# The last four row blocks of a graph-attention kernel: search order, piece size, store size and the place of four small maxima

## The chip, the cores and the metric

The kernel runs on one core of a Trainium2 chip. The metric is the device time of one launch in microseconds. The kernel before took 246.74 us (median of five runs, 246.5 to 248.25).

## What is computed

The reference is one graph-attention layer with a residual and a layer norm:

```python
ht  = (h @ W).reshape(N, 4, 512).transpose(1, 0, 2)
e   = leaky_relu(src[:, :, None] + dst[:, None, :], 0.01) + adj_mat[None]
att = softmax(e, axis=-1)
out = layernorm(h + einsum('hij,hjd->hid', att, ht).mean(axis=0))
```

Here N is 4096, h is 4096x512, adj_mat is 4096x4096, all float32. The entries of adj_mat reach 1e9, and the other term of e is small beside the gaps between a row's largest entries. In almost any row the softmax is therefore one at the row's largest adjacency entry and zero elsewhere, and the layer becomes: find the column of the largest entry of each row, fetch that row of x, multiply it by the mean of the four heads' weights, add the row's own x, and normalize.

## The kernel before, in words

`leading_rows` does this short form for all rows, and checks by the gap between a row's two largest entries that the short form holds; `general`, the full softmax, runs for blocks where it does not, behind a branch that these inputs do not take.

The rows are taken in NB = 32 blocks of 128. Row p * 32 + ib belongs to block ib and lies on partition p, so that four neighbouring blocks of x or of the output are 8 KB in one piece on each partition. A block of the adjacency is 128x4096 float32, 2 MB. For block ib the stages are:

- **Load** (`load_adj`, L105): one to four DMAs on the queue of SyncE (SP), as `pieces` (L102) says: four for blocks 0, 28 and 31, two for 29 and 30, one for the others. `LATE` is 28. Six buffers hold blocks; loads run five blocks ahead.
- **Segment maxima** (`segment_maxima`, L149): VectorE (DVE) takes the maximum of each of the 64 segments of 64 columns, by reductions over halves or quarters of the block (L155). Blocks that come in one piece are reduced in halves.
- **Segment** (`find_segment`, L160): DVE takes the eight largest of the 64 maxima and the place of the largest (L162, L164); GpSimd (POOL) turns this into a row number (L166), gathers that segment's 64 entries from the adjacency in HBM (the `lead` gather, L168), and multiplies for the column's start (L173).
- **Column** (`find_column`, L186): DVE takes the eight largest entries within the segment (`find_inner`, L184, needed only for the gap check at the very end) and the place of the largest (L190); POOL adds it to the start (L192) and gathers the row of x (the `y` gather, L178). Block 31 has its column found in the whole row (`find_column_in_row`, L198), without the lead gather, which is still made for the check.
- **Product** (`turn`, L201; `products`, L213): TensorE (PE) transposes y (L205), ScalarE (ACT) copies it out (L207), PE multiplies it by the mean weights (L218). For blocks below 28 and for 31 PE also adds the block's own x by an identity matmul (`residual`, L211).
- **Norm**: for most blocks ACT computes the sums (`stats`, L230 and L232) and applies the result (`finish`, L241), with a power on POOL for each pair of blocks (`rstd`, L235 to L237). For blocks 28 to 31 `finish_last` (L243) does it on DVE, with a square root on ACT (L254).
- **Store** (L258): on SP's queue, except the last block's, which ACT issues.

The order on each engine is the order of the program, written out by hand. Step t of the loop (L354) issues the load of block t + 5, the first part of block t's segment maxima, the column of block t - 2, the remaining maxima, the segment of block t, the product of block t - 3, the sums of block t - 4 and, on even steps, the results of blocks t - 6 and t - 5. "The first part" is `middle` quarters (L358): two in all steps but the last, one in step 31.

What comes after the loop is written out (L393 to L431): the load of x for blocks 28 to 31 in one DMA; the stores of blocks 0 to 23 in fours and of 24 and 25 singly; the column of block 30 and of block 31; then, mixed on the engines, the products of blocks 29, 30 and 31, the norms of 28 to 31, the gap check, and the stores of 26 to 31. The gap check has a scalar bound, computed in three parts (`bound`, L309): part 0 takes a maximum on DVE (L313) and transposes it on PE (L315), part 1 ends with a tiny matmul (L320), part 2 is on DVE. `test` (L327) compares on DVE, `count` (L337) sums on PE.

All DMAs issued by SP and ACT share eight completion semaphores in turn; a DMA is issued when the one eight before it has landed. The same holds for POOL's gathers with eight others.

Of the kernel before, what the change touches and what calls it, by code (L numbers as in the profile page):

```python
# [65 lines left out]
def leading_rows(ctx, tc, x, adj, W, a, out, ident, v, n_bad, any_bad):  # L66
# [7 lines left out]
    nc = tc.nc  # L74
    N, D = x.shape
    H = a.shape[0]
    KB, NB, S = D // P, N // P, N // E
    AHEAD = 5
    Q = 4
    PIECES = 4  # L80
    LATE = NB - Q
# [18 lines left out]
    adj_t = {}  # L100

    def pieces(ib):  # L102
        return PIECES if ib in (0, LATE, NB - 1) else 2 if ib > LATE else 1

    def load_adj(ib):  # L105
        if 0 <= ib < NB:
            t = adj_t[ib] = adj_pool.tile([P, N], F32, name="adj_t")
            n = pieces(ib)
            for k in range(n):
                nc.sync.dma_start(t[:, ts(k, N // n)], adj_rows[ib][:, ts(k, N // n)])  # L110

    def load_x(lo, n):
        nc.sync.dma_start(hold[:, ds(lo, n), :], x_rows[:, ds(lo, n), :])
# [35 lines left out]
    def segment_maxima(ib, lo, hi):  # L149

        if lo == 0:
            seg_of[ib] = small.tile([P, S], F32, name="seg")
        n = max(pieces(ib), 2)
        for k in range(lo * n // PIECES, hi * n // PIECES):
            nc.vector.tensor_reduce(  # L155
                seg_of[ib][:, ts(k, S // n)],
                adj_t[ib][:, ts(k, N // n)].rearrange("p (s e) -> p s e", e=E), axis=AX.X, op=OP.max,
            )

    def find_segment(ib):  # L160
        seg = seg_of.pop(ib)
        nc.vector.max(out=top[:, ib, :], in_=seg)  # L162
        at = small.tile([P, 8], U32, name="at")
        nc.vector.max_index(at, top[:, ib, :], seg)  # L164
        row = small.tile([P, 1], U32, name="row")
        nc.gpsimd.tensor_tensor(row, at[:, 0:1], first[:, ib : ib + 1], op=OP.add)  # L166
        lead = small.tile([P, E], F32, name="lead")
        nc.gpsimd.indirect_dma_start(  # L168
            out=lead, out_offset=None, in_=adj_segs,
            in_offset=bass.IndirectOffsetOnAxis(ap=row[:, :1], axis=0),  # L170
        )
        start = at_of[ib] = small.tile([P, 1], U32, name="start")
        nc.gpsimd.tensor_tensor(start, at[:, 0:1], width, op=OP.mult)  # L173
        lead_of[ib] = lead

    def gather_rows(ib, col):
        y = y_t[ib] = rows.tile([P, D], F32, name="y", bufs=4)
        nc.gpsimd.indirect_dma_start(  # L178
            out=y, out_offset=None, in_=x,
            in_offset=bass.IndirectOffsetOnAxis(ap=col[:, :1], axis=0),  # L180
        )

    def find_inner(ib):
        nc.vector.max(out=inner[:, ib, :], in_=lead_of[ib])  # L184

    def find_column(ib):  # L186
        if ib != NB - 2:
            find_inner(ib)
        within = small.tile([P, 8], U32, name="within")
        nc.vector.max_index(within, top[:, ib, :], lead_of[ib])  # L190
        col = small.tile([P, 1], U32, name="col")
        nc.gpsimd.tensor_tensor(col, at_of.pop(ib), within[:, 0:1], op=OP.add)  # L192
        gather_rows(ib, col)
# [7 lines left out]
    def turn(ib):  # L201
        y = y_t.pop(ib)
        tp = psum.tile([P, KB, P], F32, name="tp", bufs=2)
        for kb in range(KB):
            nc.tensor.transpose(tp[:, kb, :], y[:, ts(kb, P)], ident)  # L205
        yt = yt_of[ib] = rows.tile([P, KB, P], F32, name="yt")
        nc.scalar.copy(yt, tp)  # L207
# [26 lines left out]
    def rstd(i):  # L234
        nc.gpsimd.tensor_scalar(sd[:, i], sd[:, i], 1.0 / D, EPS, op0=OP.mult, op1=OP.add)  # L235
        nc.gpsimd.tensor_tensor(sd[:, i], sd[:, i], power[:, : i.stop - i.start], op=OP.pow)  # L236
        nc.gpsimd.tensor_mul(nm[:, i], nm[:, i], sd[:, i])  # L237

    def finish(ib):
        i = slice(ib, ib + 1)  # L240
        nc.scalar.activation(hold[:, ib, :], o_ps.pop(ib), AF.Identity, bias=nm[:, i], scale=sd[:, i])  # L241

    def finish_last(ib, residual):  # L243

        o = o_ps.pop(ib)
        if residual:
            nc.vector.tensor_add(hold[:, ib, :], o, hold[:, ib, :])
            o = hold[:, ib, :]
        st = small.tile([P, nc.vector.BN_STATS_DIM], F32, name="st", bufs=2)
        nc.vector.bn_stats(st, o)  # L250
        mv = small.tile([P, nc.vector.BN_AGGR_DIM], F32, name="mv", bufs=2)
        nc.vector.bn_aggr(mv, st)
        r = small.tile([P, 1], F32, name="r", bufs=2)
        nc.scalar.activation(r, mv[:, 1:2], AF.Sqrt, bias=eps)  # L254
        nc.vector.reciprocal(r, r)
        nc.vector.tensor_scalar(hold[:, ib, :], o, mv[:, 0:1], r, op0=OP.subtract, op1=OP.mult)

    def store(queue, lo, n):  # L258
        queue.dma_start(out_rows[:, ds(lo, n), :], hold[:, ds(lo, n), :])

    def mean_of_heads(kb):
        o = psum.tile([P, D], F32, name="o")
        for h in range(H):
            nc.tensor.matmul(o, ident, hold[:, w_at + kb * H + h, :], start=(h == 0), stop=(h == H - 1))  # L264
        nc.scalar.activation(w_sum[:, kb, :], o, AF.Copy, scale=1.0 / H)  # L265
# [5 lines left out]
    def turn_a():  # L271
        tp = psum.tile([P, KB, P], F32, name="tp", bufs=2)
        for k in range(KB):
            nc.tensor.transpose(tp[:, k, : 2 * H], a_rows[:, ts(k, P)], ident[: 2 * H, : 2 * H])
        nc.scalar.copy(at_d, tp[:, :, : 2 * H])

    def turn_w(kb, h):
        tp = psum.tile([P, KB, P], F32, name="tp", bufs=2)
        for k in range(KB):
            nc.tensor.transpose(tp[:, k, :], hold[:, w_at + kb * H + h, ts(k, P)], ident)  # L280
        wt = rows.tile([P, KB, P], F32, name="wt")
        nc.scalar.copy(wt, tp)  # L282
        return wt
# [25 lines left out]
    def bound(part):  # L309

        if part == 0:
            xm = once.tile([P, 1], F32, name="xm")
            nc.vector.tensor_reduce(xm, xx, axis=AX.X, op=OP.max)  # L313
            px = of_bound[0] = psum.tile([1, P], F32, name="px", bufs=1)
            nc.tensor.transpose(px, xm, ident)  # L315
        elif part == 1:
            nc.vector.tensor_reduce(xg, of_bound[0], axis=AX.X, op=OP.max)
            nc.scalar.activation(xg, xg, AF.Sqrt)
            pb = of_bound[1] = psum.tile([P, 1], F32, name="px", bufs=1)
            nc.tensor.matmul(pb, ones[0:1, :], xg, start=True, stop=True)  # L320
        else:
            nc.vector.tensor_mul(lead_by, of_bound[1], vn)
            nc.vector.tensor_scalar(lead_by, lead_by, 1.05, 110.0, op0=OP.mult, op1=OP.add)
# [28 lines left out]
    COLUMN, PROJECT, STATS, FINISH = 2, 3, 4, 6  # L352

    for t in range(NB):  # L354
        if t in x_at:
            load_x(*x_at[t])
        load_adj(t + AHEAD)
        middle = 1 if t == NB - 1 else 2  # L358
        segment_maxima(t, 0, middle)
        if t >= COLUMN:  # L360
            find_column(t - COLUMN)
        segment_maxima(t, middle, PIECES)
        pair = t >= FINISH and t % 2 == 0
        if pair:
            rstd(slice(t - FINISH, t - FINISH + 2))
        find_segment(t)
        if t < 2:
            mean_of_heads(t)
        elif t == 2:
            mean_of_heads(2)  # L370
            mean_of_heads(3)
        if t == 0:
            turn_a()
        turned = [(*vectors[0], turn_w(*vectors.pop(0))) for _ in range(vectors_at.get(t, 0))]
        if t == 16:
            head_norms()
        ib = t - PROJECT
        if ib >= 0:
            turn(ib)
            if ib < LATE:  # L380
                residual(ib)
        for some in turned:
            head_vector(*some)
        if ib >= 0:
            products(ib)
        if t >= STATS:
            stats(t - STATS)
            row_norm(t - STATS)
        if pair:
            finish(t - FINISH)  # L390
            finish(t - FINISH + 1)

    load_x(LATE, NB - LATE)  # L393
    for lo in range(0, NB - 2 * Q, Q):
        store(nc.sync, lo, Q)
    for ib in range(NB - 2 * Q, NB - FINISH):
        store(nc.sync, ib, 1)
    find_column(NB - 2)
    rstd(slice(NB - FINISH, NB - FINISH + 2))
# [4 lines left out]
    products(NB - 3, 0, KB - 1)  # L404
    finish(NB - FINISH)
    finish(NB - FINISH + 1)
    bound(0)
    finish_last(NB - 4, True)
    find_inner(NB - 2)
    find_inner(NB - 1)  # L410
    turn(NB - 2)
    products(NB - 3, KB - 1, KB)
    residual(NB - 1)
# [252 lines left out]
```

## Time and profile before

| | |
|---|---|
| median of five runs | 246.74 us |
| the profiled execution: its time / its span | 246.95 / 244.9 us |
| DVE busy | 186.3 us, 76% |
| PE busy | 201.1 us, 82% |
| ACT busy / POOL busy | 109.8 / 97.3 us |
| moved by DMA | 97.76 MB at a mean of 399 GB/s |
| segment maxima (L155) | 70 reductions, 2268 ns of a half, 1.2 us of a quarter |
| y gathers (L178) | 32, 958 ns each on POOL, 6.3 to 9.3 us from issue to landing |
| lead gathers (L168) | 32, 964 ns on POOL, 5.4 to 7.6 us to landing |
| stores of four blocks / of one block on SP's queue | 6 of 1024 KB / 7 of 256 KB |
| last instruction before the end of the span | store of block 31, issued at 239.94 us |

Times within a profile are microseconds from the start of the span. The timeline gives the start, the duration, the engine, the line and the tiles of each instruction, and in brackets how long its engine had been idle and what released it. The "DMA" row of the page gives the share of time that the 16 DMA engines were busy, in forty slices of 6.1 us.

### The profile page before, as it was taken

What the parts mean: (1) busy time and instruction counts of PE and PEld (TensorE: products, weight loads), DVE (VectorE), ACT (ScalarE), POOL (GpSimd) and SP (SyncE); (2) the same over time, 40 slices, a digit from 0 to 9 for tenths busy, and PEclk for the clock granted to TensorE, in tenths of its full rate; (3) what the DMA queues carried; (4) which work ended last, traced back from release to release, by engine and by line L of the source; (5) the groups of instructions that cost most, each with busy time, mean ns of one, the idle gap of its engine ahead of it and who ended that gap; (6) DMA issues with size and microseconds to landing.
All of it is one profiled execution on the core that took longest, in us unless ns stands there. A gap on an engine that the chain in (4) does not pass through costs nothing.

```text
span 244.9 us, 2481 instructions
## 1 busy us (share of the span) xinstructions
PE 201.1 (82%) x677; PEld 101.6 (41%) x678; DVE 186.3 (76%) x300; ACT 109.8 (45%) x266; POOL 97.3 (40%) x213
## 2 busy tenths in 40 slices
PE   0189958999999899999959979599868989858970
PEld 0035416555565555555334424243323433324520
DVE  2635785399689887999589969985998998977651
ACT  2012004055747474757646655247444845656110
POOL 1102422326425543645254636453545464742000
PEclk9999799999999999999979999799999999979997
DMA  6999999999999999999999999999999999999961
GB/s 248 439 423 412 424 427 417 422 410 423 420 412 415 411 421 420 422 402 426 424 410 419 422 419 418 408 416 415 425 409 399 407 403 406 407 425 427 412 241 55
DMA packets 13988, 97.76 MB, mean 399 GB/s; under 512 B 2184, under 2 KB 2184, under 8 KB 7824
## 3 DMA queue, kind: packets, MB, share of 16 engines
q1 hardware_dynamic: 10224, 87.82, 86.8%
q0 software_dynamic: 3584, 9.44, 9.8%
q10 hardware_dynamic: 160, 0.28, 0.3%
q8 instruction: 7, 0.11, 0.2%
q14 instruction: 13, 0.11, 0.1%
HBM read 89.15 MB, written 8.39 MB: 398 GB/s over the span
## 4 chain that ended last, share of the span: by engine, by line
issue 34%; POOL 32%; DMA 18%; PE 8%; DVE 3%; POOLq 1%; ACT 1%; SPq 1%
DMA adj_t<-in_adj_dram 15%; POOL lead L168 11%; POOL y L178 10%; PE o L218 7%; POOL sd L236 4%; DMA y<-in_x_dram,col 3%; POOL start L173 2%; POOL col L192 2%; POOL row L166 2%; DVE seg L155 2%; POOL sd L235 1%; POOL nm L237 1%; PE tp L205 1%; SPq L110 1%; ACT yt L207 0%
## 5 line engine op out<-in xcount | busy, mean ns | idle before, releaser
L155 DVE TENSOR_REDUCE seg<-adj_t 128x32 f32<-128x2048 f32 (+1 forms) x70 | 146.1, 2093 | 40.5 <-DMA adj_t<-in_adj_dram 39.8
L218 PE MATMUL o<-w_sum,yt 128*128 128x512 f32 x256 | 120.7, 613 | 1.4 <-ACT yt L207 1.4
L218 PEld LDWEIGHTS o<-w_sum,yt 128*128 128x128 f32 x256 | 47.3, 195 | 59.5 <-issue 46.9
L207 ACT COPY yt<-tp 128x512 f32<-128x512 f32 x32 | 18.8, 587 | 51.1 <-PE tp L205 51.0
L178 POOL DMA_INDIRECT y<-in_x_dram,col x32 | 30.8, 963 | 18.1 <-POOL col L192 16.0
L168 POOL DMA_INDIRECT lead<-in_adj_dram,row x32 | 32.2, 1007 | 14.0 <-POOL row L166 14.0
L205 PE MATMUL tp<-ident,y 128*128 128x128 f32 x128 | 20.4, 284 | 15.5 <-DMA y<-in_x_dram,col 15.5
L211 PE MATMUL o<-hold,ident 128*128 128x512 f32 x58 | 31.6, 628 | 0.5 <-DMA hold<-in_x_dram 0.5
L264 PE MATMUL o<-hold,ident 128*128 128x512 f32 x32 | 19.0, 750 | 15.6 <-DMA hold<-in_L_gnn_W_dram 15.6
L205 PEld LDWEIGHTS tp<-ident,y 128*128 128x128 f32 x128 | 14.8, 145 | 29.5 <-issue 27.2
L192 POOL TENSOR_TENSOR col<-start,within 128x1 uint32<-128x1 uint32 x31 | 5.8, 188 | 51.9 <-DVE within L190 51.9
L282 ACT COPY wt<-tp 128x512 f32<-128x512 f32 x16 | 9.2, 587 | 32.4 <-PE tp L280 32.4
L166 POOL TENSOR_TENSOR row<-at,first 128x1 uint32<-128x1 uint32 x32 | 6.0, 188 | 38.4 <-DVE at L164 38.4
L241 ACT ACTIVATE hold<-o,nm,sd 128x512 f32<-128x512 f32 x28 | 20.1, 769 | 0.0
L225 ACT ACTIVATE sq<-hold 128x512 f32<-128x512 f32 x32 | 19.7, 617 | 0.0
L232 ACT ACTIVATE sq<-o,nm 128x512 f32<-128x512 f32 x28 | 19.2, 687 | 0.9
L288 PEld LDWEIGHTS pv<-at_d,wt 128*128 128x128 f32 x128 | 16.3, 191 | 6.8 <-issue 3.6
L264 PEld LDWEIGHTS o<-hold,ident 128*128 128x128 f32 x32 | 7.3, 239 | 24.7 <-POOL row L166 10.8
L230 ACT ACTIVATE sq<-o 128x512 f32<-128x512 f32 x28 | 17.0, 607 | 0.0
L265 ACT ACTIVATE w_sum<-o 128x512 f32<-128x512 f32 x4 | 2.4, 598 | 32.3 <-PE o L264 32.3
L288 PE MATMUL pv<-at_d,wt 128*128 128x2 f32 x128 | 15.3, 244 | 0.6 <-ACT wt L282 0.6
L280 PEld LDWEIGHTS tp<-ident,hold 128*128 128x128 f32 x64 | 7.9, 142 | 6.9 <-issue 6.9
(73 smaller groups left out, 116.2 us busy)
## 6 DMA issues: line engine op xcount, KB each, us to landing
adj_t<-in_adj_dram SPq DMA_DIRECT2D x27, 2048.0 KB, 32.6
hold<-in_x_dram SPq DMA_DIRECT2D x7, 1024.0 KB, 33.5
adj_t<-in_adj_dram SPq DMA_DIRECT2D x12, 512.0 KB, 16.1
out_dram<-hold SPq DMA_DIRECT2D x6, 1024.0 KB, 17.5
hold<-in_L_gnn_W_dram SPq DMA_DIRECT2D x4, 1024.0 KB, 17.7
adj_t<-in_adj_dram SPq DMA_DIRECT2D x4, 1024.0 KB, 14.9
out_dram<-hold SPq DMA_DIRECT2D x7, 256.0 KB, 11.2
hold<-in_x_dram SPq DMA_DIRECT2D x4, 256.0 KB, 13.4
```

The lines of the kernel that those rows point to most:

```text
L155: nc.vector.tensor_reduce(seg_of[ib][:, ts(k, S // n)], adj_t[ib][:, ts(k, N // n)].rearrange("p (s e) -> p s e", e=E), axis=AX.X, op=OP.max,)
L168: nc.gpsimd.indirect_dma_start(out=lead, out_offset=None, in_=adj_segs, in_offset=bass.IndirectOffsetOnAxis(ap=row[:, :1], axis=0),)
L178: nc.gpsimd.indirect_dma_start(out=y, out_offset=None, in_=x, in_offset=bass.IndirectOffsetOnAxis(ap=col[:, :1], axis=0),)
L205: nc.tensor.transpose(tp[:, kb, :], y[:, ts(kb, P)], ident)
L207: nc.scalar.copy(yt, tp)
L211: nc.tensor.matmul(o_ps[ib], ident, hold[:, ib, :], start=True, stop=False)
L218: nc.tensor.matmul(o_ps[ib], yt_of[ib][:, kb, :], w_sum[:, kb, :], start=(start and kb == 0), stop=(kb == KB - 1),)
L225: nc.scalar.activation(sq, hold[:, ib, :], AF.Square, accum_out=xx[:, ib : ib + 1])
L232: nc.scalar.activation(sq, o, AF.Square, bias=nm[:, i], accum_out=sd[:, i])
L241: nc.scalar.activation(hold[:, ib, :], o_ps.pop(ib), AF.Identity, bias=nm[:, i], scale=sd[:, i])
L264: nc.tensor.matmul(o, ident, hold[:, w_at + kb * H + h, :], start=(h == 0), stop=(h == H - 1))
L288: nc.tensor.matmul(pv[:, kb, h : 2 * H : H], wt[:, k, :], at_d[:, k, h : 2 * H : H], start=(k == 0), stop=(k == KB - 1),)
```

## The change

Five edits; what each does is this.

- `pieces`: blocks 29 and 30 are loaded in four DMAs of 512 KB, not in two of 1024 KB, and so are reduced in quarters.
- `middle`: in steps 29 and 30, as in 31 before, the column of the block two steps back is looked for after the first quarter of the block's maxima, not after the first half.
- `find_column` leaves `find_inner` out for blocks 28 and 29 (as it did for 30); the inner top eights of blocks 28 to 31 are taken together after the loop.
- The stores of blocks 0 to 23 are 24 DMAs of 256 KB, not six of 1024 KB. With those of 24 and 25 that makes 26 single stores in a row.
- `finish_last` of block 28 comes before part 0 of the bound, not after it.

```diff
     def pieces(ib):
-        return PIECES if ib in (0, LATE, NB - 1) else 2 if ib > LATE else 1
+        return PIECES if ib == 0 or ib >= LATE else 1
...
     def find_column(ib):
-        if ib != NB - 2:
+        if ib < LATE:
             find_inner(ib)
...
-        middle = 1 if t == NB - 1 else 2
+        middle = 1 if t > LATE else 2
         segment_maxima(t, 0, middle)
...
     load_x(LATE, NB - LATE)
-    for lo in range(0, NB - 2 * Q, Q):
-        store(nc.sync, lo, Q)
-    for ib in range(NB - 2 * Q, NB - FINISH):
+    for ib in range(NB - FINISH):
         store(nc.sync, ib, 1)
...
     finish(NB - FINISH + 1)
+    finish_last(NB - 4, True)
     bound(0)
-    finish_last(NB - 4, True)
-    find_inner(NB - 2)
-    find_inner(NB - 1)
+    for ib in range(LATE, NB):
+        find_inner(ib)
     turn(NB - 2)
```

## The prediction, made before the change was run

> **What bounds the kernel now.** I read the page's slices first, then the waits, then the timeline of the last 45 us engine by engine.
>
> ```profile
> PE   0189958999999899999959979599868989858970
> DVE  2635785399689887999589969985998998977651
> DMA  6999999999999999999999999999999999999961
> ```
>
> The DMA engines are full in every slice but the first and the last two: up to about 212 us the adjacency arrives as fast as it can, and no edit touches that stage. What can change is the tail, from the last loads to the store at 239.94. PE's timeline there:
>
> ```profile
> 209.94 3.68 PE L218 MATMUL o<-w_sum,yt 128*128 128x512 f32 x8
> 216.41 0.63 PE L205 MATMUL tp<-ident,y 128*128 128x128 f32 x4 [2.79 <-DMA y<-in_x_dram,col]
> 217.71 5.37 PE L218 MATMUL o<-w_sum,yt 128*128 128x512 f32 x8 [0.68 <-ACT yt L207]
> 222.91 0.60 PE L205 MATMUL tp<-ident,y 128*128 128x128 f32 x4
> ...
> 226.87 0.27 PE L315 MATMUL px<-ident,xm 128*1 128x128 f32 x1
> 226.97 0.60 PE L205 MATMUL tp<-ident,y 128*128 128x128 f32 x4
> ...
> 236.46 1.12 PE L218 MATMUL o<-w_sum,yt 128*128 128x512 f32 x2
> ```
>
> PE ends block 27 at 213.62, then sits idle for 2.79 us until the y gather of block 28 lands. Its product then takes 5.37 us, not 3.68. From 216.41 PE is almost gapless to 237.58, and DVE and ACT finish block 31 in 2.4 us more. The tail is PE's, and its start is y28's landing. The stage windows say why 5.37:
>
> ```profile
> 180.10:183.50 3.40, 2.05 (x8) 1.18 (x9) 2.90 (x5) 1.35 (x4) 1.35 (x3) 1.00 1.03 419
> ...
> 214.30:217.70 3.40, 0.63 (x4) 0.42 (x4) 1.81 (x5) 0.63 (x2) 0.86 (x2) 1.00 1.04 434
> 217.70:221.10 3.40, 3.39 (x4) 1.51 (x5) 3.36 (x4) 3.37 (x11) 2.64 (x7) 0.50 1.01 424
> ```
>
> (PE's busy time is the first number after the length; the clock stands before the DMA share.) After a window with PE busy for 0.63 us, the clock is 0.50. Where y28 comes from:
>
> ```profile
> 204.95 2.29 DVE L155 TENSOR_REDUCE seg<-adj_t 128x32 f32<-128x2048 f32 x1 [0.78 <-DMA adj_t<-in_adj_dram]
> 207.16 0.22 DVE L184 MAX8 inner<-lead 128x8 f32<-128x64 f32 x1
> ...
> 207.35 0.22 DVE L190 FIND_INDEX8 within<-top,lead 128x8 uint32<-128x64 f32 x1
> 207.82 2.29 DVE L155 TENSOR_REDUCE seg<-adj_t 128x32 f32<-128x2048 f32 x1 [0.25 <-DMA adj_t<-in_adj_dram]
> 210.14 0.23 DVE L162 MAX8 top<-seg 128x8 f32<-128x64 f32 x1
> ...
> 217.74 0.09 DVE L190 MATCH_VALUE_LOAD within<-top,lead 128x8 f32 x1 [1.50 <-DMA lead<-in_adj_dram,row]
> ```
>
> The index of block 28 waits for half of block 30, which itself waits 0.78 us for its DMA, and for an inner top eight that only the final check needs. POOL issues y28 at 208.37; the DMA view gives 7.9 us to its landing. Later, DVE idles 1.50 us at 217.74 for block 30's lead gather, and everything for blocks 30 and 31 follows that.
>
> [...]y27, whose rows moved among quarter pieces, landed after 6.3 us; y28 to y31, among 1 MB transfers, after 7.9, 7.3, 7.3 and 7.9.[...] 512 KB pieces do not lower the rate (400 to 414 GB/s from 200 to 216)[...]; but the stretch 232 to 236, mostly 256 KB stores, shows 343 GB/s at a share of 0.89, or 385 at full share, against about 421 from 220 to 232.[...]
>
> **Part by part.** Times are in the profiled execution (246.95 us, span 244.9), 0.21 above the median.
>
> *Quarter instead of half, quarters of block 30, no inner top eight: y28.* DVE ends block 29's segment at about 204.17. Block 30's first half landed at 204.9; a first quarter of 512 KB comes some 1.3 us sooner (512 KB at 410 GB/s), at 203.6, so the wait of 0.78 goes. One quarter takes 1.15 (3.45 for three): done at 205.35. Block 28's lead was issued at 199.60 and took 5.6: landed at 205.2, just in time. The index is done at 205.6, against 207.57. POOL is busy with block 29's lead and start until 206.13, then adds the column (0.20) and needs the 0.53 that it shows before each gather: y28 at 206.85, 1.5 earlier. Its packets meet block 31's quarter pieces, so I take y27's 6.3 us: landed at 213.15 (7.9 would give 214.75). PE is free at 213.62: the 2.79 of idle goes, and so does the half clock (5.37 - 3.68 = 1.7). Block 28's product ends at about 218.3, not 223.07. That is 4.8 us earlier, but not the gain: the next inputs are now late.
>
> *The same edits at blocks 29 to 31.* Four quarters cost 4.6 us for two halves of 2.25, so +0.1 per block, on DVE; two inner top eights leave (0.13 each). After the index DVE does three quarters of block 30 (3.48) with data that landed by 207.8: its segment is reached at 209.1, not 210.14, 1.05 earlier. Lead30 goes out at 210.5, and with its 6.1 us lands at 216.6; DVE reaches it at about 215.3 and still waits. So block 30's index, y30 (218.85 to 217.8) and block 31's 4.42 us search (to end at 221.45), hence y31 (223.26 to 222.2), all move by 1.05. y29 (213.26 to 212.2) too. Block 29's copy on ACT is behind the four row norms of 28 to 31, which need x landed at 201.04 + 15.6 = 216.65: free at 219.5. Its first six matmuls then end at 222.75, not 227.03.
>
> *Stores of 256 KB.* [...]the trace has no gather among 2 KB rows. Bound: no help (7.3), or as much again as from 1 MB transfers to quarters (7.3 - 6.3 = 1.0), so 6.3. I take 6.3: y30 lands at 224.1 (at worst 225.1), y31 at 228.5 (at worst 230.1). Price: 24 x 256 KB = 6.3 MB at 385 instead of 421 GB/s is 16.3 instead of 14.9 us, +1.4 of DMA time. DMA was full until about 235, so it is now until 236 to 237, and the last store meets some of that: I take 0.2, between 0 and 0.6 (one 256 KB store at 410 GB/s). Eighteen more issues on SP at 0.33 each, 6 us, lie beside transfers in flight: eight are, 8 x 0.64 = 5 us of transfer.
>
> *finish_last(28) ahead of bound(0).* This orders PE too: the transpose L315 stands before block 30's transposes. DVE is free for finish_last at 221.45, and block 29's instance shows 2.66 us from its first instruction (228.47) to the next work (231.13): the maximum L313 comes at 224.1, done at 224.3, and PE's L315 and block 30's transposes (0.53 later, as in the fence: weights at 226.44, transposes at 226.97) start at about 224.9. Without this edit y30's landing (224.1 to 225.1) would decide: the edit costs 0 to 0.8. The four inner top eights then take 0.5 on DVE beside products.
>
> *Sum.* Block 30's transposes start at 224.9 instead of 226.97: 2.07 earlier. From there PE's queue is unchanged, 10.6 us to its last matmul; y31 (228.5 to 230.1) is needed at 232.21 - 2.07 = 230.14, so it just passes. Less 0.2 at the last store: 1.9. The profiled execution would take 245.05, the median **244.8**. With y30 at 225.1 the start is 225.25 and the gain 1.5; with L315 not in the way 2.7. The likeliest case: 243.9 to 245.4.
>
> **The rivals.**
>
> *Nothing gained at the end (no measurable difference): 246.3.* Little of 4.8 us at the front survives. If the late gathers keep 7.9 us, y30 lands at 225.7 and y31 at 230.1, and PE has idle stretches (219 to 220.1, 222.75 to 226) in which a window falls short of work: half clock again, 1.7 us. Then 1.2 + 0.2 - 1.7 or so leaves 0 to 0.5 of gain. For: PE's idle is moved, not removed. Against: windows with 2.05 us of PE work kept the full clock, and the tail's windows hold at least 1.6.
>
> *The full front gain carried through: 243.5.* If gathers among 2 KB rows land in 5.5 us and L313 comes sooner, the start of block 30 falls to 223.7 and the gain to 3.2. DMA's own drain, at 237 plus 2.5, forbids much more.
>
> *Slower, 251: stores held by landing.* SP issues a DMA only when the one eight before has landed (a store went out at 207.86, as the load issued at 191.76 with 16.0 us landed). Eight stores of 256 KB in flight must land in 5.1 us to keep 410 GB/s. After x's last load (216.65) 30 stores have until 242.4, where the last one lands now: 0.86 us each, or a landing of 6.9 us. The page's row for 256 KB stores says 11.2 us. At 8 us each store takes 1.0: 246.7, 4.2 us late: 251. For: that row. Against: those queued behind megabytes; the one issued at 236.48 alone took 2.1.
>
> *That the change does not do what it says* is part of the first rival: lead28 landing later than 206.45 would make DVE wait after the quarter and undo y28's and lead30's advance; it has 1.25 us of room, and lead gathers range from 5.4 to 7.6.
>
> **How the numbers follow.** Likeliest case 0.60, full gain 0.10, little gained 0.23, slower 0.07. The range must leave out no more than 0.2: it takes the full gain's 243.5 at the low end, and at the high end most of the second case, to 246.3. About 0.5% (1.2 us) can be told from no change here: faster needs 245.5. The likeliest case gives nearly all of its 0.60 and the full gain 0.10; of the little gained, 0.03 pass 245.5: 0.72 faster, 0.21 same, 0.07 slower.
>
> **What would show it.** y28 issued near 206.9 and landed before 213.7; block 28's eight matmuls in 3.7 us at clock 1.0; the idle of PE now ahead of block 30's transposes, released by L315 or y30; gathers from y29 on landing in 6.3 or less; stores 0.64 us apart. It would be wrong if DVE waits for lead28 after 205.4, if a later window of the tail shows 0.50, or if SP's stores run on past block 31's.

## The result, and the profile after

The changed kernel took 245.94 us (median of 42 runs, 244.94 to 248.36), the kernel before beside it 246.58 (79 runs, 245.72 to 249.24). The ratio is 0.9976, 95% interval 0.9964 to 0.9987: 0.24% faster, 0.6 us. The changed kernel was run twice more among the experiments, each time beside the kernel before on the same chip: 0.9938 (0.9909 to 0.9968) and 0.9944 (0.9923 to 0.9965). It is faster, by 0.2 to 0.6% in the three comparisons; 0.8% was forecast. The profiled execution took 245.59 us (span 243.7), 1.36 less than the profiled one of before. Why a profile gained twice what the first comparison did is taken up below.

The page's slices, after:

```profile
PE   0178839999999999999959876798768999886970
DMA  7999999999999999999999999999999999999992
```

DMA is now full to the last slice but one. PE's last fifteen slices have shallower holes, but more of them. PE's timeline in the tail:

```profile
209.72 0.63 PE L205 MATMUL tp<-ident,y 128*128 128x128 f32 x4 [1.16 <-DMA y<-in_x_dram,col]
...
211.05 3.68 PE L218 MATMUL o<-w_sum,yt 128*128 128x512 f32 x8
214.56 0.60 PE L205 MATMUL tp<-ident,y 128*128 128x128 f32 x4
215.84 3.70 PE L218 MATMUL o<-w_sum,yt 128*128 128x512 f32 x8 [0.68 <-ACT yt L207]
220.35 0.63 PE L205 MATMUL tp<-ident,y 128*128 128x128 f32 x4 [0.81 <-DMA y<-in_x_dram,col]
221.65 2.84 PE L218 MATMUL o<-w_sum,yt 128*128 128x512 f32 x6 [0.68 <-ACT yt L207]
224.70 0.27 PE L315 MATMUL px<-ident,xm 128*1 128x128 f32 x1 [0.20 <-DVE xm L313]
225.56 0.63 PE L205 MATMUL tp<-ident,y 128*128 128x128 f32 x4 [0.59 <-DMA y<-in_x_dram,col]
...
235.08 1.12 PE L218 MATMUL o<-w_sum,yt 128*128 128x512 f32 x2
```

The idle 2.79 us ahead of block 28 is gone, and its product takes 3.70 us, not 5.37. Part of this is luck. In this execution y27 took 7.9 us to land, where it took 6.3 before, so that PE waited 1.16 us for block 27 and ended it 1.1 us later (214.73, not 213.62). In the third profile of the changed kernel, taken among the experiments below, y27 took 6.4 us and y28 8.3, and PE does idle ahead of block 28:

```profile
216.46 0.63 PE L205 MATMUL tp<-ident,y 128*128 128x128 f32 x4 [2.07 <-DMA y<-in_x_dram,col]
```

In the first profile PE now waits for y29 (0.81) and y30 (0.59) instead. Block 30's transposes start at 225.56, 1.41 us before the old 226.97, and from there to the last matmul everything is the same. The changed kernel's stage windows (columns as before) keep the full clock here:

```profile
215.90:219.30 3.40, 3.40 (x8) 1.37 (x8) 2.71 (x8) 3.37 (x11) 1.82 (x5) 1.00 1.03 401
219.30:222.70 3.40, 1.91 (x8) 0.99 (x8) 3.37 (x3) 2.63 (x7) 1.76 (x5) 1.00 1.02 378
```

What sets y30 is seen on DVE:

```profile
205.73 0.22 DVE L190 FIND_INDEX8 within<-top,lead 128x8 uint32<-128x64 f32 x1
...
207.33 1.22 DVE L155 TENSOR_REDUCE seg<-adj_t 128x16 f32<-128x1024 f32 x1 [0.26 <-DMA adj_t<-in_adj_dram]
208.77 1.22 DVE L155 TENSOR_REDUCE seg<-adj_t 128x16 f32<-128x1024 f32 x1 [0.22 <-DMA adj_t<-in_adj_dram]
210.03 0.23 DVE L162 MAX8 top<-seg 128x8 f32<-128x64 f32 x1
...
217.15 0.09 DVE L190 MATCH_VALUE_LOAD within<-top,lead 128x8 f32 x1 [0.56 <-DMA lead<-in_adj_dram,row]
```

Block 28's index is done at 205.95, 1.6 us earlier. Yet block 30's segment is reached at 210.03, against 210.14. Before, DVE waited 0.78 and 0.25 us for the two halves of block 30; now it starts on the block sooner and waits 0.26 and 0.22 us for the third and the fourth quarter. The chain of waits of the changed kernel (start, duration, what) puts the end on y30:

```profile
218.97 6.46 DMA y<-in_x_dram,col
...
225.56 0.63 PE tp L205 x4
```

y30 was issued 0.12 us later than before, and landed after 6.5 us where it took 7.3. SP's last stores now run closer to the end, and may be the next limit. The first fence is of the kernel before, the second of the changed one, 236 to 240 us; the last two numbers are the DMA share and GB/s.

```profile
236.00:240.00 4.00, 1.59 (x5) 0.38 (x4) 2.73 (x8) 0.29 (x1) 0.00 (x0) 1.00 0.26 95
```

```profile
236.00:240.00 4.00, 0.20 (x1) 0.00 (x0) 1.86 (x4) 0.29 (x1) 0.00 (x0) 0.98 0.70 264
```

### The profile page after: what moved, and what is told of

It is laid out like the page before. It is cut to its first block, busy times and chain, and to the rows that moved or that the text cites. A ratio compares the mean times of both kernels' runs of the same rounds, so it can differ in the third digit from the quotient of the medians.

```text
span 243.7 us, 2526 instructions
## 1 busy us (share of the span) xinstructions
PE 195.9 (80%) x677; PEld 98.6 (40%) x678; DVE 186.5 (77%) x304; ACT 109.9 (45%) x266; POOL 97.2 (40%) x213
## 4 chain that ended last, share of the span: by engine, by line
issue 37%; POOL 34%; DMA 18%; PE 4%; DVE 3%; POOLq 1%; SPq 1%; ACT 0%
DMA adj_t<-in_adj_dram 15%; POOL lead L168 11%; POOL y L178 11%; POOL sd L236 4%; PE o L218 3%; DMA y<-in_x_dram,col 3%; POOL start L173 2%; POOL col L192 2%; POOL row L166 2%; DVE seg L155 2%; POOL sd L235 1%; POOL nm L237 1%; SPq L110 1%; PE tp L205 0%; POOLq L178 0%
## 5 line engine op out<-in xcount | busy, mean ns | idle before, releaser
L218 PE MATMUL o<-w_sum,yt 128*128 128x512 f32 x256 | 118.4, 603 | 1.4 <-ACT yt L207 1.4
L218 PEld LDWEIGHTS o<-w_sum,yt 128*128 128x128 f32 x256 | 45.8, 190 | 57.4 <-issue 44.5
L205 PE MATMUL tp<-ident,y 128*128 128x128 f32 x128 | 19.8, 277 | 16.8 <-DMA y<-in_x_dram,col 16.6
L264 PE MATMUL o<-hold,ident 128*128 128x512 f32 x32 | 18.0, 714 | 18.6 <-DMA hold<-in_L_gnn_W_dram 18.6
L211 PE MATMUL o<-hold,ident 128*128 128x512 f32 x58 | 29.7, 593 | 0.0
L205 PEld LDWEIGHTS tp<-ident,y 128*128 128x128 f32 x128 | 14.2, 142 | 31.1 <-issue 27.8
## 6 DMA issues: line engine op xcount, KB each, us to landing
hold<-in_x_dram SPq DMA_DIRECT2D x4, 256.0 KB, 13.3
```

The costliest lines, as they stand in the source:

```text
L211: nc.tensor.matmul(o_ps[ib], ident, hold[:, ib, :], start=True, stop=False)
L218: nc.tensor.matmul(o_ps[ib], yt_of[ib][:, kb, :], w_sum[:, kb, :], start=(start and kb == 0), stop=(kb == KB - 1),)
```

## The experiments

All ratios are to the kernel before on the same chip, with 95% intervals. Edits are against the kernel before unless said otherwise.

### First four: the change taken apart

**Stores alone.**

```diff
-    for lo in range(0, NB - 2 * Q, Q):
-        store(nc.sync, lo, Q)
-    for ib in range(NB - 2 * Q, NB - FINISH):
+    for ib in range(NB - FINISH):
         store(nc.sync, ib, 1)
```

> The kernel before with the 26 single stores and nothing else of the change. Theory A (the gain is the landing of the last gathers among smaller stores; the earlier search for block 28 gives nothing that lasts, because block 30's lead gather is set by the arrival of block 30): the whole gain of the change, 0.4 to 0.8 us under the kernel before, y30 and y31 landing within 6.6 us of their issue where they took 7.3 and 7.9. Theory B (the gain is block 28's earlier search, which removes PE's idle stretch and the half clock behind it): 0 to 0.2 us, whatever the gathers do.

Measured: 246.16 against 246.94, 0.9988 (0.9963 to 1.0013). y28 to y31 land after 6.9, 6.7, 5.9 and 5.9 us. The landings are as theory A has them, and in its profile block 30's transposes start at 225.69 though its block 30 arrives 1 us later (208.87) than in the profile of before, as its block 28 does already. That profile has only 0.62 us of idle ahead of block 28, as y27 came late in it (7.6 us). The time doesn't show it beyond its interval: no clear gain.

**All but the stores.** Against the changed kernel:

```diff
-    for ib in range(NB - FINISH):
+    for lo in range(0, NB - 2 * Q, Q):
+        store(nc.sync, lo, Q)
+    for ib in range(NB - 2 * Q, NB - FINISH):
         store(nc.sync, ib, 1)
```

> The changed kernel with the stores of blocks 0 to 23 in fours again. Theory A: little of the gain is left, within 0.2 us of the kernel before on average, y30 to y31 landing after 7.3 us or more, PE waiting for y30. Theory B: 0.4 us or more under the kernel before.

Measured: 247.12, 1.0020 (0.9996 to 1.0044). No gain. In this kernel's PE timeline the idle stretch has moved from block 28 to block 29, whose gather took 8.9 us (7.3 in another profile with these transfers, "All but the stores, PE kept busy" below):

```profile
215.08 3.70 PE L218 MATMUL o<-w_sum,yt 128*128 128x512 f32 x8 [0.68 <-ACT yt L207]
221.83 0.63 PE L205 MATMUL tp<-ident,y 128*128 128x128 f32 x4 [3.05 <-DMA y<-in_x_dram,col]
223.13 4.47 PE L218 MATMUL o<-w_sum,yt 128*128 128x512 f32 x6 [0.68 <-ACT yt L207]
```

Its windows show the half clock moved with it:

```profile
219.60:223.00 3.40, 0.63 (x4) 0.42 (x4) 3.37 (x3) 0.51 (x3) 1.39 (x5) 1.00 1.01 425
223.00:226.40 3.40, 3.27 (x4) 1.51 (x5) 1.77 (x9) 1.61 (x4) 0.79 (x1) 0.50 1.01 419
```

So theory B falls: the early search alone carries nothing to the end. Theory A isn't enough either, since the stores alone have no clear gain.

**The order of the bound.** Against the changed kernel:

```diff
-    finish_last(NB - 4, True)
     bound(0)
+    finish_last(NB - 4, True)
```

> The changed kernel with part 0 of the bound ahead of the norm of block 28 again. In the changed kernel's profile PE's small transpose is done 0.6 us before y30 lands, so both theories expect the changed kernel's time within 0.15 us; the prediction's step, in which this order costs up to 0.8 us, expects it up to 0.8 us faster than the changed kernel.

Measured: 245.43, 0.9943 (0.9918 to 0.9969); the changed kernel itself had 0.9938 and 0.9944 on two other chips, each beside the kernel before. No cost of this order is seen.

**PE kept busy in the kernel before.**

```diff
         ib = t - PROJECT
+        if t == NB - 1:
+            pf = psum.tile([P, P], F32, name="px", bufs=1)
+            for _ in range(12):
+                nc.tensor.matmul(pf, ident, ident, start=True, stop=True)
         if ib >= 0:
             turn(ib)
```

> The kernel before with twelve extra matmuls of the identity with itself (about 2.6 us, into a scratch tile) in PE's queue ahead of block 28's transposes, so that the stretch of idle before them is filled and the clock stays up in every execution. The output is unchanged. It tells what the half clock costs the kernel before: PE then waits for y30, which lands at 226.1, instead of reaching it late at 226.97. Theory A: 0 to 0.9 us under the kernel before, as often as the half clock falls there. Theory B: 0.5 us or more, most of the change's gain.

Measured: 246.67, 0.9996 (0.9976 to 1.0016). Inconclusive: in its profile block 27's product ended at 215.3 only, so the 2.84 us of extra matmuls held block 28's transposes to 217.98, about 2 us past y28's landing (208.94 + 6.9), and gave back what the clock had saved (3.70 us for the product).

### Next four: pieces against search, and y30 taken away

**The changed kernel again.**

> The changed kernel itself, beside the next three on the same chip. Both theories: about 0.6 us under the kernel before (ratio 0.9976 so far). It is the base against which the others are read, and its profile shows whether y30's 6.5 us to landing, and block 30's last quarter landing 13.9 us after block 28's, come again.

Measured: 245.80 against 247.09, 0.9938 (0.9909 to 0.9968). A store goes out on SP when the DMA eight before has landed (207.86 after 207.80 in the profile of before, 207.37 after 207.31 in the changed kernel's first), so SP's issue times tell the landings: block 30's last piece 13.97 us after block 28's last (195.08 to 209.05), against 13.36 before (194.50 to 207.86). PE waits for y30 again (0.44).

**Stores and pieces, the search late.** As the stores alone, and

```diff
-        return PIECES if ib in (0, LATE, NB - 1) else 2 if ib > LATE else 1
+        return PIECES if ib == 0 or ib >= LATE else 1
```

> The kernel before with single stores and with blocks 29 and 30 in four pieces; the search stays behind the half. Theory P (the small pieces themselves cost transfer time): block 30's last piece lands about 13.9 us after block 28's last, as in the changed kernel, not 13.36 as with halves, and the time is 0.3 to 0.6 us above the stores alone. Theory G (the early gather, in front of the adjacency's last pieces, takes their place): 13.4 us, and the time of the stores alone.

**Stores and early search, halves loaded.** As the stores alone, and

```diff
-        n = max(pieces(ib), 2)
+        n = PIECES if ib >= LATE else max(pieces(ib), 2)
...
-        middle = 1 if t == NB - 1 else 2
+        middle = 1 if t > LATE else 2
```

> The kernel before with single stores, the search in steps 29 to 31 after the first quarter, and blocks 29 and 30 loaded in halves but reduced in quarters. Theory P: block 30's last half lands 13.4 us after block 28's last piece, and the time is at or up to 0.5 us under the stores alone. Theory G: 13.9 us, and no gain over the stores alone.

Measured, landings of block 30's and block 31's last pieces after block 28's last:

| kernel | block 30 | block 31 | ratio |
|---|---|---|---|
| before | 13.36 | 19.27 | 1 |
| stores alone | 13.36 | 19.26 | 0.9988 (0.9963 to 1.0013) |
| stores and pieces | 14.17 | 19.90 | 0.9997 (0.9963 to 1.0030) |
| stores and early search | 13.69 | 19.59 | 0.9988 (0.9971 to 1.0005) |
| changed, again | 13.97 | 19.89 | 0.9938 (0.9909 to 0.9968) |

Both theories hold in part. With the DMA engines full (a 9 in 38 of the 40 slices of the changed kernel's page), the smaller pieces put block 31's arrival back by 0.6 us, and the early search without them, which issued y28 at 207.88 and not at 209.37 as in the stores alone, by 0.3; together it is 0.6. The distances for block 30 come back in all 18 profiles of this case: 13.3 to 13.4 us with halves and the late search (four profiles), 14.1 to 14.2 with pieces and the late search (three), 14.0 with pieces and the early search (ten). Block 28's own last piece lands anywhere from 194.4 to 195.9 us in them, whatever the edit. No time follows from that: the runs of stores and pieces fell into four at 244.8 to 245.1 and ten at 246.9 to 248.5. The profile is of one of the four, at 245.13; its windows show why it could be otherwise:

```profile
213.40:216.80 3.40, 0.79 (x5) 0.42 (x4) 2.41 (x5) 0.03 (x1) 0.61 (x2) 1.00 1.00 392
216.80:220.20 3.40, 2.79 (x7) 1.36 (x8) 2.60 (x4) 3.37 (x10) 2.63 (x6) 1.00 1.05 408
```

PE is busy for 0.79 us in 3.4, as little as where the clock fell to half in other profiles (0.63 in before's and in that of all but the stores), and here it didn't fall. That made theory H of the next runs: whether the clock falls to half after such a stretch is chance, and the early search is worth what it spares of that.

The clock records of the traces show how. In each of the 18 profiles all changes of the clock lie whole multiples of 3.413 us apart: in before's they stand at 26.54, 29.96, 125.53, 128.94, 156.25, 159.66, 217.69 and 221.10 us, which is 1, 28, 1, 8, 1, 17 and 1 times 3.413. This grid stands differently in nearly every execution. In the profile of stores and pieces the changes at 157.29, 181.18 and 239.21 us put two windows of the grid at 211.90 and 215.31, and PE's idle stretch is shared between them:

```profile
211.90:215.31 3.41, 1.66 (x4) 0.38 (x2) 3.25 (x3) 1.25 (x2) 1.62 (x4) 1.00 1.03 408
215.31:218.72 3.41, 1.94 (x7) 1.09 (x8) 1.77 (x8) 1.92 (x6) 1.50 (x5) 1.00 1.02 396
```

PE was busy for 1.66 and 1.94 us of these windows, and both were followed by full clock, as all windows with more than 1.51 us were between 46 and 236 us (last section). The record also has the mean granted clock of every run: 0.956 for the ten long runs of stores and pieces, 0.971 for the four short ones. By estimate one half-clock window takes 0.007 off it (0.5 x 3.41 / 245). But none of the ten was profiled, two of them have 0.971 or more, and the medians of the groups lie 2.6 us apart where the half clock added 1.7 us to block 28's product before. So the clock is seen in the split, and whether it is all of it stays open.

Stores and early search lack what the changed kernel gains: the intervals don't meet. In that profile y28 was issued at 207.88, 0.6 us later than in the changed kernel beside it, took 8.3 us, and PE idled 2.13 us ahead of block 28. What the pieces add to the early search was not tried further.

**y30 at once.** The changed kernel without the gather of block 30 by its own column: it takes block 29's, one step earlier, so block 30's rows are not the reference's.

```diff
-        gather_rows(ib, col)
+        if ib != NB - 2:
+            gather_rows(ib, col)
+        if ib == NB - 3:
+            gather_rows(NB - 2, col)
```

> The changed kernel with block 30's rows of x gathered by block 29's columns, right after block 29's own gather, so that PE never waits for the index of block 30; this leaves the right rows of block 30 out. If y30's landing sets the end, as the chain of the changed kernel's profile says, PE's transposes of block 30 come at about 223 instead of 225.6, and the time falls by 1.0 to 1.8 us, until y31 (landing near 229) or the stores' drain at 238 takes over. If y30 was only the last of several equal waits, by less than 0.4 us.

Measured: 245.25 against 245.80 for the changed kernel, 0.9914 (0.9886 to 0.9943). The gain is half of what was expected, with overlapping intervals. PE's timeline of this kernel (its lines are three further down) shows the next wait at once:

```profile
224.98 0.27 PE L318 MATMUL px<-ident,xm 128*1 128x128 f32 x1 [0.85 <-DVE xm L316]
225.09 0.62 PE L208 MATMUL tp<-ident,y 128*128 128x128 f32 x4
```

It is the maximum behind `finish_last` of block 28. So y30 decides by some 0.7 us only (225.81 to 225.09). PE ended 0.74 us earlier than in the changed kernel beside it, but the span (243.9 and 243.8) did not.

### The clock, and mixed stores

**Stores and pieces, PE kept busy.** As stores and pieces, and in the place of the twelve matmuls above

```diff
+        if t == NB - 1:
+            pf = psum.tile([P, P], F32, name="px", bufs=1)
+            for _ in range(6):
+                nc.tensor.matmul(pf, ident, ident, start=True, stop=True)
```

> Single stores and four pieces, the search still late, with six extra matmuls of the identity with itself (about 1.4 us, scratch result) in PE's idle stretch ahead of block 28's transposes; the output is unchanged. Theory H (the early search is worth only what the half clock costs: in the kernel with stores and pieces alone PE idles 2.5 us there[...], which makes its runs split into some at 245.1 and most near 247.5): the runs no longer split, and the median falls to 245.2 to 245.8. Rival (the split has another cause): still split, median above 246.5.

Measured: 245.45 against 247.19, 0.9934 (0.9912 to 0.9956). Without the extra matmuls it was 0.9997 (0.9963 to 1.0030): the intervals don't meet. The runs lie from 244.7 to 247.0, 17 of 18 under 246.2. PE's timeline:

```profile
213.40 1.50 PE L381 MATMUL px<-ident 128*128 128x128 f32 x12
216.32 0.63 PE L205 MATMUL tp<-ident,y 128*128 128x128 f32 x4 [1.43 <-DMA y<-in_x_dram,col]
217.63 3.70 PE L218 MATMUL o<-w_sum,yt 128*128 128x512 f32 x8 [0.68 <-ACT yt L207]
```

y28 still lands late, and nothing of the search was moved. Useless work in the gap is worth as much here (0.9934) as the early search (0.9938 for the changed kernel).

**Stores alone, PE kept busy.** The same six matmuls on the stores alone.

> The kernel before with single stores and with the six extra matmuls ahead of block 28's transposes, no edit of the search or the pieces; the output is unchanged. Theory H: as good as the whole change, 0.3 to 0.6% under the kernel before, without a second group of slow runs. Rival: as the stores alone, ratio 0.9988.

Measured: 245.95, 0.9962 (0.9941 to 0.9984), against 0.9988 (0.9963 to 1.0013) without them. It goes as theory H has it, though the intervals overlap.

**All but the stores, PE kept busy.** As all but the stores, and

```diff
         row_norm(ib)
+    pf = psum.tile([P, P], F32, name="px", bufs=1)
+    for _ in range(6):
+        nc.tensor.matmul(pf, ident, ident, start=True, stop=True)
     turn(NB - 3)
```

> All of the change but the stores, with six extra matmuls ahead of block 29's transposes, where PE idled 3.05 us and the clock was at half afterwards; the output is unchanged. Theory H: block 29's first six matmuls take 2.84 and not 4.47 us, block 30's transposes then wait for y30 at about 226.5, and the ratio to the kernel before falls from 1.002 to 0.998 to 1.000. Rival: it stays at 1.002.

Measured: 247.13, 0.9999 (0.9972 to 1.0025). In the profile the first six product matmuls of block 29 take 2.84 us, and block 30's transposes wait 1.00 us for y30, to 226.23. So the product is no longer slowed (4.47 us without the extra matmuls); that the time moved from 1.0020 isn't beyond its interval. With 1 MB stores neither run shows a gain.

**Mixed stores.** The version with the bound first, and

```diff
-    for ib in range(NB - FINISH):
+    for ib in range(14):
         store(nc.sync, ib, 1)
+    for lo in range(14, NB - FINISH, Q):
+        store(nc.sync, lo, Q)
```

> The changed kernel with part 0 of the bound first, and with single stores only for blocks 0 to 13, those that move while gathers are under way; blocks 14 to 25 again in fours. Theory D (SP's stores, whose last packet came at 239.4 to 239.7, are the next limit beside y30): their last packet comes 0.5 to 0.9 us earlier, block 31's store takes its 1.0 us alone, and the time is 0 to 0.4 us under the 245.4 to 245.8 of the changed kernel's family. Rival (the megabyte stores delay y31 again, landing after 7 us): at or above the changed kernel.

Measured: 246.09, 0.9970 (0.9941 to 0.9999). SP's last store ends as expected (last packet 238.64, against 239.36), without a gain. Its profile caught the half clock in what is otherwise the changed kernel, y28 having taken 7.9 us:

```profile
212.50:215.90 3.40, 1.16 (x6) 0.42 (x4) 2.88 (x5) 0.70 (x3) 0.96 (x1) 1.00 1.01 407
215.90:219.40 3.50, 3.43 (x4) 1.51 (x5) 2.77 (x6) 3.47 (x12) 2.35 (x5) 0.51 1.04 403
```

So the early search doesn't exclude the half clock. That it makes it rarer is inferred from the run times: on the chip where both ran, one of nine runs of the changed kernel took over 247 us, and nine of the fourteen of stores and pieces.

### The last four

**The changed kernel, PE kept busy**, where `keep_busy` is four of the matmuls above, and stands a third time ahead of block 28's transposes:

```diff
         row_norm(ib)
+    keep_busy()
     turn(NB - 3)
     products(NB - 3, 0, KB - 1)
+    keep_busy()
     finish(NB - FINISH)
```

**The changed kernel** a third time, and **stores and pieces, PE kept busy**, again, both without an edit.

> The changed kernel with four extra identity matmuls (0.9 us) each ahead of block 28's transposes, ahead of block 29's and behind block 29's first six product matmuls; the output is unchanged. If the half clock still falls into the changed kernel's idle stretches in some executions: 0.3 to 0.8 us under the changed kernel's median beside it, with less spread. If not: within 0.2 us of it, or above it by what the extra matmuls cost.

> The changed kernel as the base of the other three on this chip: 0.2 to 0.7% under the kernel before.

> Single stores and four pieces, search late, six extra matmuls ahead of block 28's transposes, as run before at a ratio of 0.9934. If the early search has a value of its own beyond the clock: 0.2 us or more above the changed kernel with PE kept busy. If the clock is all of its value: the same as that one, or better.

Measured against 247.30: 246.44 and 0.9962 (0.9942 to 0.9982); 245.99 and 0.9944 (0.9923 to 0.9965); 245.56 and 0.9938 (0.9920 to 0.9956). The first does not answer its question: the third group of extra matmuls stands right in front of L315 (L320 in that kernel), which starts at 226.87, so the extra work lies on the path itself; how often the half clock still falls in the changed kernel stays open. The last repeats its 0.9934 and is level with the changed kernel (0.9938 and 0.9944 in the later two comparisons): beside a PE that is kept busy no value of the early search itself is seen.

**y30 at once, mixed stores**: the two edits shown above on the changed kernel.

> Block 30's rows gathered by block 29's columns at once (which leaves the right rows of block 30 out), and blocks 14 to 25 stored in fours. In the run with single stores, PE ended 0.7 us earlier than in the changed kernel, yet the span did not end earlier, as block 31's store took 2.0 us beside SP's last stores and not 1.0. If the drain was that wall: SP's last packet 0.6 to 0.9 us earlier than 239.7, block 31's store at 1.0 us, and 0.4 to 1.0 us under the version with single stores (245.25). If not: the same as it.

Measured: 0.9922 (0.9889 to 0.9955), level with 0.9914 for single stores. In its profile SP's last packet came at 238.79, not 239.68, block 31's store took its usual 1.0 us of packets where it had taken 2.0, and the span was 242.6, not 243.9. One profile speaks for the drain as the wall behind y30; the medians don't, and it stays open.

## Why the prediction was partly right, and what failed

The direction, the place of the new waits and the effect of the stores were right; the size was not: 1.9 us forecast, 1.36 between the two profiles, 0.6 between the medians.

*y28.* Forecast issued at 206.85 and landed at 213.15; it was issued at 206.99 and took 7.0 us. Its product took 3.70 at full clock, as forecast, though with luck: the forecast took y27's 6.3 us among the quarter pieces as what such pieces allow, and y27 itself took 7.9 us among them in this execution. Which gather is late varies (last section), so the landing was not set by the size of the pieces alone.

*The step that failed: "three quarters of block 30 (3.48) with data that landed by 207.8".* The 1.05 us by which lead30, y30 and y31 were to move came from it. Block 30's segment was reached at 210.03, not 209.1. Lead30 was issued at 211.44 instead of 211.55, y30 later than before (218.97, forecast 217.8), and only y31 earlier (by 0.58). The arrival was held fixed while two edits touched what arrives: block 30's last piece landed at 208.8. Of this 1.0 us, 0.6 is what small pieces and earlier gathers cost with the engines full, as the table of landings shows; by 0.4 block 28 was late already. (The prediction had read off the trace that 512 KB pieces do not lower the rate. Block 31's 0.6 us says otherwise.) Block 28's index was late too (205.95, not 205.6), but the arrival came last. What remained was the landing: y30 took 6.5 us (forecast 6.3), 0.8 us less than before. So block 30's transposes waited for y30, not for L315, and started at 225.56, not 224.9: this took some 0.5 of the 1.9 us away.

*The half clock, counted once and for all.* Before's profiled execution had it, and it delayed block 30's transposes there: y30 landed at 218.85 + 7.3 = 226.15, and with the 0.14 us that the chain shows between landing and transposes they could have started at 226.3, not 226.97. That is 0.7 of the 1.36 us. An execution of before without the half clock has only some 0.65 to lose, which is what the medians of the first comparison differ by. In the later two the changed kernel stood at 245.80 and 245.99, where it had been, and before at 247.09 and 247.30, 1.3 above it: it is before that varies, as it would if it met the half clock more often there. The granted clocks speak for it: over 213 executions of the kernel before, run beside the experiments, the longer half has 0.958 in the mean and the shorter half 0.966, about one half-clock window apart (0.007 by the estimate above).

I took one execution's clock for the kernel's; the grid, and the split of stores and pieces, ended by 1.5 us of useless matmuls, show that it is a chance. How large a chance can be estimated by sliding the grid over a profiled PE timeline and counting the positions that leave a window in the tail with under 1.4 to 1.5 us of work, where the windows counted in the last section part: 83 to 88% for before, 75 to 81% for stores and pieces (26 to 32% and none in its two profiles with PE kept busy), none for the first two profiles of the changed kernel, 61 to 67% for the third. That this makes up the whole distance between profile and medians is argued, not shown: the run made to show it on the kernel before filled the gap too far.

*The stores.* That smaller stores let the late gathers land sooner was my estimate, from one gather among quarter pieces (y27, 6.3 us). It was right in sign and place, and the gain hangs on them: without them the rest gains nothing. In the profile y29 to y31 took 7.1, 6.5 and 6.4 us, where 6.3 or less was named as a sign. But alone they gain nothing clear either. With PE's gap filled, or with pieces and the early search together, they do; with the early search over halves no gain was seen. The drain was undersized: forecast full until 236 to 237, while the last SP store, issued at 235.59, took 4.3 us (2.1 before). The 0.2 us for its meeting the last store was not needed in the profile, whose last store took 2.5 us as before.

*finish_last ahead of bound(0).* Forecast L315's successor at about 224.9; with y30 out of the way it started at 225.09. As the edit of the order is hidden behind y30, it cost nothing.

*Two sums.* For the first rival, 1.2 + 0.2 - 1.7 is -0.3, not the 0 to 0.5 that it was said to leave; and the 2.7 with L315 out of the way leaves out the 0.2 at the last store.

## What to carry to other kernels

With the transfers full, the earlier gather and the smaller pieces were paid for here by another arrival (0.6 us of block 31's); work out whose before taking credit for an earlier start. A stretch of 3.4 us with PE busy for 0.63 us was followed by the half clock in before's profile, and one with 0.79 us was not in that of stores and pieces: whether a stall cost a half clock was a distribution here, and one profile shows one draw of it, so price the gain with and without. And six useless matmuls (1.50 us) in the gap took stores and pieces from 0.9997 to 0.9934; they ended before the awaited data landed and stood off the path. Twice here they did not, and no gain came of them.

## What the runs showed that was not expected

Among 256 KB stores y30 and y31 landed after 5.6 to 6.7 us (the eight profiles of single stores that show both), against 7.3 to 8.0 among 1 MB stores (four profiles).

Counted in the grid's own windows from 46 to 236 us, 951 windows at full clock in the 18 profiles, the half clock follows PE's busy time closely in this kernel and its variants. Each of the 28 windows with PE busy for at most 1.38 of 3.41 us was followed by half clock, none of the 918 with more than 1.51 us was, and of the five between two were. In before's profile the three are 122.12 to 125.53 (0.45 us busy), 152.84 to 156.25 (1.02) and 214.28 to 217.69 (0.63); in the changed kernel's first there is none, and 178.36 to 181.77, with 1.41, was followed by full clock. In the first 46 us windows with up to 3.1 us busy were followed by half clock too (2.56 us, 23.13 to 26.54, in before's), so busy time is not all that counts there.

In 17 of the 18 profiles one of the gathers y26 to y29 is seen to take 7.6 to 8.9 us: y27 in seven, y28 in eight, and differently in executions of one kernel. A late y27 holds PE up ahead of block 27 and leaves little or no gap ahead of block 28 (0 and 0 us in the first two profiles of the changed kernel); a late y28 opens that gap (2.07 us in the third). The runs do not show what makes a gather late.
